# Own messages of a graph layer: from their own matmuls to scaled rows of x added to the slot sums in PSUM

## The chip, the core and the metric

The kernel runs on one core of a Trainium2 chip. The metric is device microseconds from the first to the last instruction of that core, as the hardware profiler takes it. The engines are called PE (matrix unit), PEld (its weight loads), DVE (vector), ACT (scalar), POOL (general, here the issuer of gathers) and SP (here the issuer of plain DMAs).

## The reference

N = 50,000 nodes carry rows of D = 160 numbers (64 scalars, 32 vectors of three). E = 1,650,000 edges have a source, a target and NK = 4 attributes. The edges are sorted by target, and each node has exactly one edge to itself among them, its "own" edge: 50,000 of the 1,650,000. A message is bilinear in the source's row and the edge's four attributes; messages are summed by target, mixed by two small matrices, and the layer ends in a residual, a relu and a layer norm:

```
out0 = C0 * (ss * e0 @ W1 + dot * INV3 @ W2)
...
m_agg = segment_sum(m, dst, num_segments=n)
hs = m_agg[:, :64] @ Ws * LIN_S
...
h  = concat([hs, hv])
x  = layernorm(x + x + relu(h))
```

Because a message is linear in the source's row for each attribute, the whole of it is the sum over k of attribute k times (row of x) times a fixed 160 x 160 matrix B_k, into which the W's are folded. So rows of x scaled by an attribute may be summed by target first, once for each k, and be multiplied by B_k afterwards.

## The kernel before, in words

**Edges and slots.** The sorted edges are cut into units of 128. G = 6 units make a group, whose targets span at most W = 32 consecutive nodes from the group's base (its first target). A group's sums live in one half of a PSUM tile ps: 128 partitions are 4 attributes x 32 slots, the 160 columns are the features. Two groups are a pair (PG = 2), four groups a chunk (QG = 4), 20 groups a super-chunk (SG = 20, ten pairs). There are 2,087 groups, 1,044 pairs, 522 chunks, 105 super-chunks and 391 blocks of 128 nodes.

**The main loop** runs over pairs. For each pair:
- POOL issues 12 indirect DMAs (gather, L324), each of which brings 128 rows of x into a slice of the tile xg. The pool of xg has four buffers of one pair, so POOL may run four pairs ahead of PE.
- DVE builds ha for the next pair (spread, L333 and L336): for each edge a one-hot over 32 slots times its four attributes.
- PE does 12 matmuls ps += ha^T xg (group_sums, L362). An f32 matmul appears as two weight loads and two passes.
- DVE transposes the finished ps by 32 x 32 blocks into the chunk's tile sums (turn_sums, L372), one pair later, after the second matmul of the next pair.

After a chunk, PE multiplies sums by the folded matrix in five matmuls (apply_weights, phc, L603), which gives 128 rows hp of the transformed sums by slot. When all chunks that can touch a block of 128 nodes are there, PE adds their hp to the block's nodes by one-hot matmuls (block, phb, L684), and DVE and ACT do the relu, residual and norm (L186 to L200). SP stores the output, two blocks at a time (L812).

**Own edges.** From the hundredth group on (head of 100 groups excepted), own edges are taken out of the edge list before gathering: "packs" of 128 long rows of raw edges are read, their own edges are found on DVE, the rest is squeezed together (many steps on DVE, L470 to L551), and SP writes it to a DRAM tensor edges. The four attributes of each node's own edge are written to a DRAM tensor selves, 4 numbers a node, at an address that is held in a register (put, L586). The super-chunks then read edges (load, L255).

The own messages come back in with the blocks. For each pair of blocks SP reads the rows of x (xt, L624) and their shares (sa, L628) seven pairs ahead of the chunk that completes the block. For each block PE transposes xt in two halves (turned, L650), ACT copies them to xT (L653), PE multiplies xT by the four B_k (own, yx, eight matmuls, L665), and DVE scales each product by its share and sums them up into t (L671, L673). At the end t is added to phb (L686).

**Order.** The order on SP, PE, DVE and ACT is that of the program text (manual_schedule). Work beside the 12 matmuls of a pair is held in a list of tasks with a first pair (after_pair, hand_over); after each matmul of the main loop, work(1.0) lets about one matmul's worth of tasks follow. The steps of a pack are spread evenly up to a due pair. PSUM tiles of phc, ptx, yx and phb share two buffers (psM, tag misc).

Of the kernel before, what the change touches and what calls it, by code (L numbers as in the profile page):

```python
# [50 lines left out]
P = 128  # L51
# [54 lines left out]
def tile_gnn_resnorm(ctx: ExitStack, tc: tile.TileContext, x, src, dst, attr, W1, W2, W3, W4, W5, Ws, Wv, out, n_edges):  # L106
# [104 lines left out]
    cuts = sorted({0, NH // QG, NCH} | {round(i * NCH / 10) for i in range(10)})  # L211
    bounds = []
    for c0, c1 in zip(cuts, cuts[1:]):
        t = min((near(c) / N for c in range(c0, c1 + 1)), key=lambda t: abs(t - 0.5))
        off = 5 * math.sqrt(n_edges * max(0, t * (1 - t))) / (degree - 1) + 10
        bounds += [(-off, 0.75 * step + W + off)] * (c1 - c0)
# [9 lines left out]
    with tc.tile_pool(name="once", bufs=1) as once, tc.tile_pool(name="raw", bufs=2) as rawp, \  # L226
# [4 lines left out]
            tc.tile_pool(name="ahead", bufs=5) as aheadp, tc.tile_pool(name="outs", bufs=3) as outp, \  # L231
# [3 lines left out]

        extremes = once.tile([P, 2, NSC], F32, name="extremes")
        baseB = once.tile([P, NCH * QG], F32, name="baseB")
# [41 lines left out]
        def place(cast_):  # L279
# [9 lines left out]
            nc.vector.tensor_scalar(baseB[:, gs], bank[:, 3, :ng], float(N - 1), None, op0=ALU.min)  # L289
            for g in range(QG):  # L290
                r = slice(g * W, (g + 1) * W)
                for c0, c1, h in ((s * SG // QG, (s * SG + ng) // QG, g),
                                  ((s * SG + ng) // QG, math.ceil((s * SG + ng) / QG), min(g, ng % QG - 1))):
                    if c0 < c1:
                        nc.vector.tensor_scalar(rowid[r, c0:c1],
                                                baseB[r, c0 * QG:c1 * QG].rearrange("p (c g) -> p c g", g=QG)[:, :, h],
                                                pidx[r], float(-g * W), op0=ALU.add, op1=ALU.add)
            yield 1
# [18 lines left out]
            placed[s] = si, rel, pk  # L317

# [51 lines left out]
        def turn_sums(ps, ng, at, i):  # L370

            nc.vector.transpose(at[:, :, i:i + ng, :].rearrange("p b g w -> p g b w"),  # L372
                                ps[:, :ng].rearrange("p g (b f) -> p g b f", f=FB))
# [14 lines left out]
        selves = dram.tile([1, (row_start(NR - 1)[1][1] + W) * NK], F32, name="selves")  # L388
# [4 lines left out]
        def row_table(tmp):  # L393
# [9 lines left out]
            nz = math.ceil((row_start(0)[1][1] + W) / P)  # L403
# [215 lines left out]
        def ahead(bs):  # L619
# [6 lines left out]
            assert rows_stored[0] == NR or row_start(rows_stored[0])[1][0] >= n1  # L626
            sa = aheadp.tile([P, BP, NK], F32, name="sa")
            dq.dma_start(sa[:nb, :len(bs)],  # L628
                         selves[0, n0 * NK:n1 * NK].rearrange("(h n k) -> n h k", h=len(bs), k=NK))
            return [(xt[:, h], sa[:, h]) for h in range(len(bs))]  # L630
# [11 lines left out]
        H = D // 2  # L642

        def turned(b, xt, sa):

            nb, row = rows_of(b)
            pt = psM.tile([H, 2, P], F32, name="ptx", tag="misc")
            fresh("misc")
            for i in range(2):
                wrote("misc", nc.tensor.transpose(pt[:, i, :nb], xt[:nb, i * H:(i + 1) * H], ident[:nb, :nb]))  # L650
                yield 0.75
            xT = np_.tile([H, 2, P], F32, name="xT")
            evict(xT[:, :, :nb], pt[:, :, :nb])  # L653
            return xt, sa, xT

        def own(b, xt, sa, xT):

            nb, row = rows_of(b)
            t = aheadp.tile([P, D], F32, name="t")
            for h in range(NK // 2):  # L660
                y = psM.tile([P, 2, D], F32, name="yx", tag="misc")
                fresh("misc")
                for k in range(2):
                    for i in range(2):
                        wrote("misc", nc.tensor.matmul(y[:nb, k], xT[:, i, :nb], BWh[:, i, 2 * h + k, :],  # L665
                                                       start=i == 0, stop=i == 1))
                        yield 1
                for i in range(2):
                    k = 2 * h + i
                    if k == 0:  # L670
                        nc.vector.tensor_scalar(t[:nb], y[:nb, i], sa[:nb, 0:1], None, op0=ALU.mult)  # L671
                    else:
# [425 lines left out]
```

## Time and profile before

| | |
|---|---|
| median of 3 runs | 18,558.09 us (18,557.72 to 18,613.09) |
| profiled execution | 18,571.46 us |
| its span | 18,569.1 us, mean granted PE clock 0.665 |
| PE busy | 8,634.2 us (46%), 41,633 passes |
| PEld busy | 7,746.4 us (42%), 41,634 |
| DVE busy | 6,447.4 us (35%), 11,070 |
| ACT busy | 486.0 us (3%) |
| POOL busy | 11,887.8 us (64%), 12,536 |
| DMA | 797,538 packets, 1,215.93 MB, mean 65 GB/s; software queue 20.7% of 16 engines, SP's queue 3.3% |

A row of the page's fifth part reads: line, engine, operation, tile written <- tiles read, count | busy us in total, mean ns of one | idle us of that engine just before them, and what ended the most of it ("issue": nothing that the profile shows; "remote": a semaphore whose raiser it can't name). A row of a timeline reads: start in us, duration in us, engine, line, operation, tiles, count, and in brackets the engine's idle time before it. SPq are issues of DMAs by SP; SP's register moves and loads are not in the page's busy time. Utilization is even over the span: in each of the 40 slices PE shows 4 or 5 tenths, POOL 6, DMA 2.

### The profile page before, as it was taken

How to read it: one execution, taken by the hardware profiler on the slowest of the kernel's cores; microseconds unless marked ns; L12 is line 12 of the kernel's file. 1: busy time of each engine (PE TensorE's matmuls, PEld its weight loads, DVE VectorE, ACT ScalarE, POOL GpSimd, SP SyncE). 2: the span in 40 equal slices, each digit the busy share in tenths (PEclk: the TensorE clock that was granted, in tenths of full speed). 3: DMA queues.
4: the chain of work that ended last, by engine and by line, in shares of the span. 5: the costliest groups of instructions: out<-in, count | busy, mean ns of one | idle time of the engine just before them, and what ended most of it. 6: DMA issues, size and time to landing. Idle time of an engine off the chain costs nothing.

```text
span 18569.1 us, 122717 instructions
## 1 busy us (share of the span) xinstructions
PE 8634.2 (46%) x41633; PEld 7746.4 (42%) x41634; DVE 6447.4 (35%) x11070; ACT 486.0 (3%) x1392; POOL 11887.8 (64%) x12536
## 2 busy tenths in 40 slices
PE   4444444444444444444445444455444444444444
PEld 3434444443443444444344444444444444344434
DVE  4332433423333233332333334233342423324222
ACT  0000000000000000000000000000000000000000
POOL 6666666666666666666666666666666666666665
PEclk6666666666666666666666666666666666666666
DMA  2222222222222222222222222222222222222222
GB/s 69 71 61 71 63 65 67 62 71 60 66 69 61 72 62 67 67 63 70 61 65 70 62 71 63 72 63 66 70 63 71 61 71 61 63 69 61 65 62 54
DMA packets 797538, 1215.93 MB, mean 65 GB/s; under 512 B 271491, under 2 KB 575800, under 8 KB 792918
## 3 DMA queue, kind: packets, MB, share of 16 engines
q0 software_dynamic: 601056, 1026.60, 20.7%
q1 hardware_dynamic: 194410, 180.15, 3.3%
q8 instruction: 330, 5.41, 0.1%
q14 instruction: 302, 2.47, 0.0%
q10 hardware_dynamic: 1440, 1.29, 0.0%
HBM read 1135.77 MB, written 71.40 MB: 65 GB/s over the span
## 4 chain that ended last, share of the span: by engine, by line
another core or an unknown queue 41%; issue 18%; PE 17%; DVE 10%; POOL 9%; ACT 1%; DMA 1%; DVEq 0%; SPq 0%; ACTq 0%; POOLq 0%
PE ps L362 9%; POOL xg L324 9%; PE phb L684 3%; DVE ha L336 2%; PE phc L603 2%; PE yx L665 2%; DVE hot L333 1%; DVE prow L534 1%; DVE sums L372 1%; DMA xg<-in_x,si 1%; DVE t L673 1%; DVE hot L638 0%; PE ptx L650 0%; DVE t L671 0%
## 5 line engine op out<-in xcount | busy, mean ns | idle before, releaser
L324 POOL DMA_INDIRECT xg<-in_x,si x12522 | 11883.6, 949 | 6638.9 <-issue 3628.4
L362 PE MATMUL ps<-xg,ha 128*128 128x160 f32 x25044 | 6522.3, 364 | 3418.1 <-issue 3062.0
L362 PEld LDWEIGHTS ps<-xg,ha 128*128 128x128 f32 x25044 | 5110.6, 241 | 3852.5 <-issue 3457.2
L372 DVE STREAM_TRANSPOSE sums<-ps 128x320 f32<-128x320 f32 x1044 | 534.2, 512 | 5451.7 <-remote 4041.4
L665 PE MATMUL yx<-BWh,xT 80*128 80x160 f32 x6256 | 1792.5, 364 | 880.7 <-issue 824.7
L684 PE MATMUL phb<-hp,hot 128*128 128x160 f32 x3474 | 1151.0, 422 | 2225.5 <-ACT xT L653 1099.2
L603 PE MATMUL phc<-BWk,sums 128*128 128x160 f32 x5220 | 1353.5, 343 | 1065.3 <-DVE t L673 534.0
L336 DVE TENSOR_TENSOR ha<-hot,pk 128x1536 f32<-128x1536 f32 x1044 | 1830.2, 1753 | 35.7
L684 PEld LDWEIGHTS phb<-hp,hot 128*128 128x128 f32 x3474 | 854.3, 280 | 2342.9 <-ACT xT L653 1144.9
L665 PEld LDWEIGHTS yx<-BWh,xT 80*128 80x128 f32 x6256 | 1344.0, 241 | 1004.7 <-issue 942.0
L603 PEld LDWEIGHTS phc<-BWk,sums 128*128 128x128 f32 x5220 | 1020.7, 225 | 1128.2 <-DVE t L673 563.5
L673 DVE SCALAR_TENSOR_TENSOR t<-yx,sa,t 128x160 f32<-128x160 f32 x1173 | 449.5, 383 | 2274.5 <-remote 1734.2
L671 DVE TENSOR_SCALAR t<-yx,sa 128x160 f32<-128x160 f32 x391 | 148.6, 380 | 1917.8 <-remote 1692.6
L650 PE MATMUL ptx<-ident,xt 128*80 128x128 f32 (+1 forms) x782 | 202.6, 351 | 1294.2 <-DVE t L673 982.2
L686 DVE TENSOR_TENSOR phb<-phb,t 128x160 f32<-128x160 f32 x391 | 128.1, 328 | 1687.3 <-remote 1000.5
L650 PEld LDWEIGHTS ptx<-ident,xt 128*80 128x80 f32 (+1 forms) x782 | 92.6, 142 | 1374.0 <-DVE t L673 1038.2
L333 DVE TENSOR_TENSOR hot<-bank,rel 128x384 f32<-128x384 f32 x1044 | 551.5, 528 | 34.1 <-PE ps L362 31.8
L534 DVE COPY_PREDICATED prow<-marks,prow 128x2370 f32<-128x2370 int32 (+8 forms) x160 | 445.9, 2787 | 1.2
L607 ACT COPY hp<-phc 128x160 f32<-128x160 f32 x522 | 152.8, 293 | 9795.3 <-remote 5044.4
L653 ACT COPY xT<-ptx 80x256 f32<-80x256 f32 x391 | 143.9, 368 | 8133.0 <-remote 4941.6
L534 DVE COPY_PREDICATED pra<-marks,pra 128x1580 f32<-128x1580 int32 (+8 forms) x160 | 306.5, 1915 | 0.0
L300 PE MATMUL bank<-ident,r 120*128 120x120 f32 x100 | 46.0, 460 | 542.0 <-DVE baseB L289 398.3
(144 smaller groups left out, 3035.8 us busy)
## 6 DMA issues: line engine op xcount, KB each, us to landing
xg<-in_x,si POOLq DMA_INDIRECT x12522
edges<-prow SPq DMA_DIRECT2D x1994, 18.5 KB
r<-edges SPq DMA_DIRECT2D x99, 360.0 KB
selves<-mine SPq DMA_DIRECT2D x1992, 0.5 KB
xt<-in_x SPq DMA_DIRECT2D x195, 160.0 KB
out<-o SPq DMA_DIRECT2D x195, 160.0 KB
pra<-in_attr SPq DMA_DIRECT2D x15, 1580.0 KB
pri<-in_src SPq DMA_DIRECT2D x15, 395.0 KB
```

The lines of the kernel that those rows point to most:

```text
L324: got.append(nc.gpsimd.indirect_dma_start(out=xg[:, j, :], out_offset=None, in_=x, in_offset=bass.IndirectOffsetOnAxis(ap=placed[0][:, u + ...
L333: nc.vector.tensor_tensor(hot[:, :n], slotsP[:, 0:W].unsqueeze(1).to_broadcast([P, n, W]), rel[:, u:u + n].unsqueeze(2).to_broadcast([P, n ...
L336: nc.vector.tensor_tensor(ha[:, :n], hot[:, :n].unsqueeze(2).to_broadcast([P, n, NK, W]), pk[:, :, u:u + n].rearrange("p k u -> p u k").un ...
L362: mm = nc.tensor.matmul(ps[:, j // G, :], ha[:, j].rearrange("p k w -> p (k w)"), xr, start=j % G == 0, stop=j % G == G - 1)
L372: nc.vector.transpose(at[:, :, i:i + ng, :].rearrange("p b g w -> p g b w"), ps[:, :ng].rearrange("p g (b f) -> p g b f", f=FB))
L534: nc.vector.copy_predicated(what[:n, a:e], mi[:, r].unsqueeze(2).to_broadcast([n, e - a, what.shape[2]]), what[:n, a + d:e + d])
L603: wrote("misc", nc.tensor.matmul(ph[:ng * W], at[:, b, :ng].rearrange("p g w -> p (g w)"), BWk[:, b, :], start=b == 0, stop=b == ND - 1))
L607: evict(hp[:ng * W], ph[:ng * W])
L650: wrote("misc", nc.tensor.transpose(pt[:, i, :nb], xt[:nb, i * H:(i + 1) * H], ident[:nb, :nb]))
L665: wrote("misc", nc.tensor.matmul(y[:nb, k], xT[:, i, :nb], BWh[:, i, 2 * h + k, :], start=i == 0, stop=i == 1))
L673: nc.vector.scalar_tensor_tensor(t[:nb], y[:nb, i], sa[:nb, k:k + 1], t[:nb], op0=ALU.mult, op1=ALU.add)
L684: wrote("misc", nc.tensor.matmul(ph[:nb], hot2[:r, i, :nb], hp[:r], start=i == 0, stop=i == len(cs) - 1))
```

## The change

Own messages leave the blocks and join the groups. In ps, partition (k, w) holds attribute k times rows of x summed for the node base + w. The own message of that node is its share k times its row of x; so a tile xr whose partition (k, w) holds row base + w of x, four times over, scaled by a column that holds share k of node base + w, is just what has to be added to ps. A node may lie in two groups' spans; its share counts only in the last, that is where base + w is below the next group's base (keep_shares), and is zero in the column elsewhere.

- turn_sums first calls add_own: for each group of the pair one DVE operation ps = xr * share + ps, in PSUM, then the transpose as before.
- ask_near: at the end of the step of pair p, SP asks for xr of pair p + 2: one register load of two addresses, and for each group one DMA of 32 rows of x, broadcast to four copies. Four buffers.
- ask_shares: once per super-chunk SP loads the addresses and issues one DMA of 128 single numbers for each group, handed over five pairs into the super-chunk before; keep_shares on DVE follows two pairs later.
- bases, in place: three DVE operations per super-chunk that turn the bases into byte addresses; the registers are loaded from there.
- Gone: turned, own, the reads of sa, the sum t and its addition to phb. The reads of xt come two pairs ahead of the completing chunk instead of seven.
- The due pair of a pack is also held before the first shares that need it. One more check on the widest step between bases, and somewhat wider bounds for the last chunk.

In all the program issues 1,988 DMAs of xr, 1,988 of shares (at) and 1,294 register loads for them on SP, and 1,988 operations of add_own on DVE; it loses 3,128 matmuls yx, 782 transposes, 391 copies xT, 1,564 operations on t, 391 additions to phb and 196 reads of sa.

```diff
-            nc.vector.tensor_scalar(baseB[:, gs], bank[:, 3, :ng], float(N - 1), None, op0=ALU.min)
+            nc.vector.tensor_scalar(baseB[:, gs], bank[:, 3, :ng], float(N - W), None, op0=ALU.min)
...
+            bases(s)
...
+        def bases(s):
+
+            g0, g1 = s * SG, min(NG, (s + 1) * SG)
+            lo, hi = reach(g0)[0], reach(g1)[1]
+            f = idxp.tile([1, SG], F32, name="basef")
+            i = basep.tile([1, 2, SG], I32, name="basei")
+            nc.vector.tensor_scalar(f[:, :g1 - g0], baseB[0:1, g0:g1], float(lo), float(hi), op0=ALU.max, op1=ALU.min)
+            for t, width in enumerate((NK, D)):
+                nc.vector.tensor_scalar(i[:, t, :g1 - g0], f[:, :g1 - g0], float(4 * width), None, op0=ALU.mult)
+            bases_[s] = i
+
+        def at_base(s, t, u0, u1):
+            _, v = nc.values_load_multi_w_load_instructions(
+                bases_[s][0:1, t, u0:u1], engines=[ET.SP], min_val=0, max_val=(N - W) * 4 * (NK, D)[t],
+                skip_runtime_bounds_check_because="held within bounds")
...
+        def ask_shares(s):
+
+            g0, g1 = counted(s)
...
+            at = sharep.tile([P, SG + 1], F32, name="at")
+            runs = [(s - 1, SG - 1, SG)] if g0 < s * SG else []
+            runs += [(s, u, min(u + 10, g1 - s * SG)) for u in range(0, g1 - s * SG, 10)]
+            i = 0
+            for s_, u0, u1 in runs:
+                for v in at_base(s_, 0, u0, u1):
+                    dq.dma_start(at[:, i:i + 1].bitcast(U8),
+                                 self_bytes[ds(v, W * 4 * NK)].rearrange("(w k b) -> k w b", k=NK, b=4))
+                    i += 1
+            shares[s] = at
+
+        def keep_shares(s):
...
+            nc.vector.memset(kept, 0.0)
+            nc.vector.scalar_tensor_tensor(keep[:, :n], baseB[:, g0 + 1:g1 + 1], slot_of[:, 0:1], baseB[:, g0:g1],
+                                           op0=ALU.subtract, op1=ALU.is_gt)
+            nc.vector.copy_predicated(kept[:, :n], keep[:, :n], shares[s][:, :n])
...
+        def ask_near(p):
+
+            s, g, ng = pairs[p]
+            own = [i for i in range(ng) if g + i >= OWN]
+            if not own:
+                return
+            xr = nearp.tile([P, PG, D], F32, name="xr")
+            for i, v in zip(own, at_base(s, 1, g + own[0] - s * SG, g + ng - s * SG)):
+                rows = xbytes[ds(v, W * 4 * D)].rearrange("(w b) -> w b", w=W)
+                dq.dma_start(xr[:, i, :].bitcast(U8), rows.unsqueeze(0).to_broadcast([NK, W, 4 * D]))
+            near_[p] = xr
...
+        def add_own(p, ps):
+
+            s, g, ng = pairs[p]
+            xr = near_.pop(p, None)
+            for i in range(ng):
+                if g + i >= OWN:
+                    share = next(shares.pop((t, g + i)) for t in (s, s + 1) if (t, g + i) in shares)
+                    nc.vector.scalar_tensor_tensor(ps[:, i], xr[:, i], share, ps[:, i], op0=ALU.mult, op1=ALU.add)
...
-        def turn_sums(ps, ng, at, i):
-
+        def turn_sums(p, ps, ng, at, i):
+
+            add_own(p, ps)
             nc.vector.transpose(at[:, :, i:i + ng, :].rearrange("p b g w -> p g b w"),
                                 ps[:, :ng].rearrange("p g (b f) -> p g b f", f=FB))
...
-        def turned(b, xt, sa):
...
-        def own(b, xt, sa, xT):
...
-            nc.vector.tensor_tensor(ph[:nb], ph[:nb], t[:nb], op=ALU.add)
...
-            due.append((first - 1) * per - 1)
+            own = next(s for s in range(NH // SG, NSC) if i * RP and reach(min(counted(s)[1], NG - 1))[1] + W > row_start(i * RP)[1][0] or not i * RP)
+            due.append(min((first - 1) * per - 1, (own - 1) * per + 4))
...
-        AHEAD = 7
+        AHEAD = 2
...
-                after_pair(max(at - AHEAD + 3, START), do_turned, b)
-                after_pair(max(at - AHEAD + 5, START + 2), do_own, b)
...
+                if counted(s + 1)[0] < counted(s + 1)[1]:
+                    after_pair(p + 5, ask_shares, s + 1)
+                    after_pair(p + 7, keep_shares, s + 1)
...
-            turning = ps, ng, sums, g % QG
-            fetch(p)
+            turning = p, ps, ng, sums, g % QG
+            if p + 2 < len(pairs):
+                ask_near(p + 2)
```

## The prediction

> **What bounds the kernel now.** I read the page first, then the timelines of POOL, PE and SP in the middle of the run, then counted instructions between the stalls seen there. The page's rows:
>
> ```profile
> L324 POOL DMA_INDIRECT xg<-in_x,si x12522 | 11883.6, 949 | 6638.9 <-issue 3628.4
> L362 PE MATMUL ps<-xg,ha 128*128 128x160 f32 x25044 | 6522.3, 364 | 3418.1 <-issue 3062.0
> L665 PE MATMUL yx<-BWh,xT 80*128 80x160 f32 x6256 | 1792.5, 364 | 880.7 <-issue 824.7
> L673 DVE SCALAR_TENSOR_TENSOR t<-yx,sa,t 128x160 f32<-128x160 f32 x1173 | 449.5, 383 | 2274.5 <-remote 1734.2
> L686 DVE TENSOR_TENSOR phb<-phb,t 128x160 f32<-128x160 f32 x391 | 128.1, 328 | 1687.3 <-remote 1000.5
> ```
>
> The first row sets the floor. Its busy and idle time make 18,522 of the span's 18,569 us. A gather costs 0.949 us and, when nothing holds it, an "issue" gap of 3,628.4 us / 11,880 = 0.305 us: 12,522 x 1.254 = 15,703 us. The remaining 18,522 - 15,703 = 2,819 us are stalls of POOL. No saving on another engine is worth more than these 2,819 us, and the change leaves the 12,522 gathers alone. When do they occur? POOL's timeline, the gathers with a long wait:
>
> ```profile
> 8017.20 0.95 POOL L324 DMA_INDIRECT xg<-in_x,si  x1 [4.76 <-remote]
> 8051.93 0.95 POOL L324 DMA_INDIRECT xg<-in_x,si  x1 [4.68 <-remote]
> 8086.40 0.95 POOL L324 DMA_INDIRECT xg<-in_x,si  x1 [4.71 <-remote]
> ```
>
> Every 34.5 us, two pairs of groups, POOL stands 4.7 us at the first gather of a pair. It waits for one of the four buffers xg, which PE frees with a pair's last matmul. Nearly all of some 600 such stalls stand at that place. So PE is late; PE's timeline in the middle one of these cycles says how:
>
> ```profile
> 8042.91 0.42 PE L362 MATMUL ps<-xg,ha 128*128 128x160 f32 x1 [2.39 <-issue]
> 8045.01 0.42 PE L362 MATMUL ps<-xg,ha 128*128 128x160 f32 x1 [1.68 <-issue]
> 8047.84 0.42 PE L665 MATMUL yx<-BWh,xT 80*128 80x160 f32 x1 [2.40 <-issue]
> 8049.25 0.43 PE L665 MATMUL yx<-BWh,xT 80*128 80x160 f32 x1 [0.99 <-issue]
> ...
> 8052.04 0.74 PE L362 MATMUL ps<-xg,ha 128*128 128x160 f32 x2
> 8052.57 0.74 PE L665 MATMUL yx<-BWh,xT 80*128 80x160 f32 x2
> ```
>
> Until 8050 PE crawls: starts lie at multiples of 0.70 us, with no operand missing (its gathers had been issued some 40 us earlier). From 8051 it runs a pass each 0.27 us. DVE's transpose at 8051.69 waited for a PE group whose last matmul is recorded at 8033, so PE's completions were held too. The crawl ends about 4.3 us after POOL has stopped. SP is caught in it as well; its own timeline:
>
> ```profile
> 8245.75 0.23 SPq L586 DMA_DIRECT2D selves<-mine  x1
> 8246.07 0.36 SPq L586 DMA_DIRECT2D edges<-prow  x1
> ...
> 8255.75 0.69 SPq L586 DMA_DIRECT2D edges<-prow  x1
> 8257.16 0.70 SPq L586 DMA_DIRECT2D selves<-mine  x1
> ```
>
> What starts a crawl? Not an idle PE: most start in the midst of work. I counted instructions from the end of one crawl to the start of the next, in 197 such stretches: a straight fit gives each PE instruction 0.0071 and each SP instruction 0.0072 of a stretch, that is some 140 of either. Stretches with many on SP (mean 34) had 105 on PE; those with few (2) had 134. DMA packets weigh nothing in it. I take this as a budget of instructions per stretch: the cause is not shown, the count is.
>
> **The change part by part.** *PE.* It loses 3,128 matmuls of yx and 782 transposes: 6,256 + 782 matmul rows and as many weight loads, 14,076 of 83,267. Their busy time, 1,792.5 + 202.6 us, lies under POOL and is worth nothing directly. Also gone are PE's waits for the evicted xT and for t (rows of phb and ptx: some 1 ms each), which lie in the same shadow. *ACT* loses 391 copies of xT, 143.9 us, hidden.
>
> *DVE.* Out: 391 + 1,173 on t and 391 on phb, 148.6 + 449.5 + 128.1 = 726 us. In: 1,988 scaled additions on PSUM. No row has PSUM as both source and target with an SBUF operand; nearest is L673, 383 ns, same form and size: 761 us. Bounds are 328 ns (L686, in place in PSUM) and 405 (the normalization's L200, two operands from SBUF): 652 to 805 us. Per super-chunk eight or nine small operations at 0.15 to 0.28 us, about 0.2 ms over 105. Net +0.24 ms (0.13 to 0.28) on a DVE that is 35% busy. It lengthens the step from a group's last matmul to its transpose by 2 x 0.38 us per pair; PE has a whole pair to do meanwhile. Nothing on the path, if the rows are there.
>
> *SP and its queue.* In: 1,988 reads of x rows (82 KB each, four copies), 1,988 reads of shares (128 numbers of 4 bytes), 1,294 register loads, and a register move for each read; out: 196 reads of sa. Durations in the trace: a move 29 ns, the issue of xt 415 ns and of sa 485 ns (256 rows each), of a store 227 ns; a load of 16 registers 1.15 us, of one 0.36. So 3,976 x (0.26 to 0.52) + 1,294 x (0.36 to 0.7) = 1.5 to 3.0 ms on an SP that spends 2.8 ms now: hidden in 18.5 ms while it keeps up. It does pass r, xt, out and the packs' stores in one queue; r has some four pairs of lead, xt six, the others need none. The new reads have less: asked for two pairs ahead (x rows), two to three (shares). Behind a late one stand DVE's addition, the transpose and the next pair's spread, and behind that PE.
>
> *DMA engines.* The rows are 163 MB on 1,216. Here the Trainium skill speaks against the change. "DMA: Bandwidth & Descriptors", section "Rules for kernel authors", says that an outermost dimension below 16, such as a leading broadcast of c copies, confines a DMA to c engines; both new reads lead with 4. By the trace's packets, 640 bytes take 36 ns and small ones 9: 128 x 45 ns x 1,988 = 11.5 ms of engine time. Over 16 engines that is 0.7 ms each; by the rule four of them get 2.9 ms each, 15% above the 24% they have now. A read then lands 1.2 us later than a spread one, against a lead of two pairs. Either way not a bound; I add nothing.
>
> A second rule, "TensorE: Matmul & The Clock Gate", section "HAM oscillation", says that gaps throttle the clock; fewer matmuls leave more gaps. The granted clock is already 0.665. Were all of the 34,600 passes that stay at the half-clock pace of 0.266 us, they would take 9.2 ms; the sum stays the same.
>
> *The stalls.* PE and SP have 84,403 + 9,984 = 94,387 instructions now (PE's 1,137 semaphore waits included). Change: -14,076 on PE, +2 x 3,976 + 1,294 - 196 = +9,050 on SP: 89,361, 5.3% fewer. With a fixed budget per stretch the stalls fall in proportion: 2,819 x 0.053 = 149 us. Both ends: nothing, if a stall comes every two pairs because four buffers fill; and 2,819 x 0.169 = 476 us, if only PE's count matters. I take the middle one, for SP's weight was measured.
>
> **Sum.** The profiled execution took 18,571 us (span 18,569), 13 above the median of 18,558. 18,571 - 149 = 18,422; against the median 18,409. I say **18,410 us**, 0.8% faster.
>
> **Rivals.** *A, the budget, as above:* 18,410, own range 18,330 to 18,520. Chance 0.35.
>
> *B, PE is the matter.* If crawls depend on PE alone, 18,558 - 476 = 18,080; and if PE also gets through three pairs instead of two before a crawl, since its back-and-forth with ACT and DVE for own messages is gone, one stall of 4.7 us falls on three pairs: 1.6 us a pair in place of 2.7, 1,044 x 1.1 = 1.2 ms less, 17,400. For it: rows with millisecond waits on xT and t. Against it: over windows of six pairs, pair time shows no trend with yx passes (17.8 us at 5.3 passes a pair, 17.5 between 6.7 and 8, 18.3 at 8). Chance 0.17.
>
> *C, SP's queue becomes a stage: slower.* Once in ten pairs the shares of a super-chunk are asked for in one lump: 20 x 2 + 3 = 43 instructions, 10 us when SP is free, 43 x 0.70 = 30 us in a crawl, plus 2 us to land. DVE takes them two to three pairs on: 35 us at the mean pace, but 14 to 16 us when PE and DVE do two pairs in one burst. It decides once the lump outlasts that: then DVE stands some 16 us, and PE and POOL after it. In half of the 99 super-chunks that is 0.8 ms: 19,240 with A's gain; in all, 20,060. Packs' stores (33 instructions a step) ahead of the x rows do the same. For it: crawls fill half of the time. Against it: pairs in which SP has 16 stores, far more than the 4 new reads, take only 0.3 us longer (18.0 against 17.7). Chance 0.33.
>
> *D, no effect:* a stall is fixed by the four buffers and comes every two pairs anyway. 18,560. For it: 435 of 604 intervals between stalls are two pairs. Chance 0.15.
>
> **Range and chances.** A measurement of this kernel tells about 0.3%, 56 us, from no change. A falls nearly all to faster, B wholly, D to the same, C to slower but for a little: 0.50, 0.17, 0.33. The range, 17,500 to 19,350, leaves out B's end and C's full price, under 2 in 10.
>
> **What would show it.** Right if POOL's mean stays at 949 ns and its idle falls by about 150 us; if PE has 69,190 matmuls and loads and its crawls stay; if ps<-xr takes near 383 ns and doesn't wait for DMA. B shows as stalls three pairs apart. C shows as DVE's additions or the copy of the shares idle until a DMA of xr or at. The forecast is wrong at the root if the gathers themselves get slower, say by sharing four DMA engines, or if crawls vanish: then 15.7 ms is open.

## The result: 1.3% slower

The changed kernel took 18,816.49 us (median of 4 runs, 18,809.39 to 18,828.72), the kernel before 18,557.9 (4 runs, 18,546.59 to 18,613.09): ratio 1.0134, interval 1.0113 to 1.0155. The forecast was 18,410, faster. The page of the changed kernel, parts 2, 3 and 5:

```profile
DMA packets 1269269, 1379.65 MB, mean 73 GB/s; under 512 B 488595, under 2 KB 1047368, under 8 KB 1264614
...
q1 hardware_dynamic: 666106, 344.04, 6.9%
...
L417 POOL DMA_INDIRECT xg<-in_x,si x12522 | 11848.7, 946 | 6923.1 <-issue 3621.3
L455 PE MATMUL ps<-xg,ha 128*128 128x160 f32 x25044 | 6560.4, 380 | 8374.5 <-issue 6584.8
...
L410 DVE SCALAR_TENSOR_TENSOR ps<-xr,kept,ps 128x160 f32<-128x160 f32 x1988 | 769.8, 387 | 6932.8 <-remote 2488.4
```

Read the POOL row first, as before. A free gather costs 0.946 + 0.305 = 1.251 us, so the floor is 12,522 x 1.251 = 15,665 us; busy and idle make 18,771.8, and the difference is stalls: 3,107 us, against 2,819 in the kernel before. The whole loss is stall time of POOL (the floor itself is 38 us lower). The additions take 387 ns each. PE lost all its yx rows, yet its idle time of kind "issue", the crawl, grew. New on the page are the packets: SP's queue q1 went from 194,410 to 666,106.

By the gathers' start times the changed kernel has 592 stalls of 5.25 us in the mean where the kernel before has 605 of 4.66. Of 9 us or more there are 26 (405 us in all) in place of one (11 us), so the shorter ones fell, from 2,808 us to 2,702. Within the 45 us before 24 of the 26, DVE's longest wait for a transfer or for ScalarE had been at x rows or at the step that takes up the shares. One of them, in the timelines of DVE and then of POOL:

```profile
4103.69 0.39 DVE L410 SCALAR_TENSOR_TENSOR ps<-xr,kept,ps 128x160 f32<-128x160 f32 x1 [10.93 <-DMA xr<-in_x]
...
4121.68 0.39 DVE L410 SCALAR_TENSOR_TENSOR ps<-xr,kept,ps 128x160 f32<-128x160 f32 x1 [0.58 <-DMA xr<-in_x]
```

```profile
4130.27 0.95 POOL L417 DMA_INDIRECT xg<-in_x,si  x1 [0.30 <-issue]
4144.55 0.94 POOL L417 DMA_INDIRECT xg<-in_x,si  x1 [13.34 <-PE ps L455]
```

DVE stands 10.9 us for x rows that SP asked for at 4100.18, behind a pack's stores; POOL pays some 40 us later. The table of waits of the same kernel adds such places up (us in total, times, longest us):

```profile
POOL xg L417 <- PE ps L455: 2216.6, 359, 40.2
DVE ps L410 <- DMA xr<-in_x: 1634.5, 224, 33.1
...
DVE kept L382 <- DMA at<-selves: 469.1, 15, 45.7
```

That is rival C's sign, word for word. The experiments say that it is a part of the cause and not the whole.

### The profile page after: what moved, and what is told of

Read it like the earlier page. It is cut to its first block, busy times and chain, and to the rows that moved or that the text cites. A ratio compares the mean times of both kernels' runs of the same rounds, so it can differ in the third digit from the quotient of the medians.

```text
span 18809.7 us, 120151 instructions
## 1 busy us (share of the span) xinstructions
PE 7544.6 (40%) x34595; PEld 6677.7 (36%) x34596; DVE 6577.2 (35%) x11924; ACT 358.3 (2%) x1001; POOL 11853.5 (63%) x12540
## 5 line engine op out<-in xcount | busy, mean ns | idle before, releaser
L455 PE MATMUL ps<-xg,ha 128*128 128x160 f32 x25044 | 6560.4, 380 | 8374.5 <-issue 6584.8
L455 PEld LDWEIGHTS ps<-xg,ha 128*128 128x128 f32 x25044 | 5258.0, 252 | 9091.9 <-issue 7164.2
L410 DVE SCALAR_TENSOR_TENSOR ps<-xr,kept,ps 128x160 f32<-128x160 f32 x1988 | 769.8, 387 | 6932.8 <-remote 2488.4
L697 PE MATMUL phc<-BWk,sums 128*128 128x160 f32 x5220 | 1306.2, 327 | 854.8 <-issue 854.1
L186 DVE SCALAR_TENSOR_TENSOR y<-phb,xt 128x160 f32<-128x160 f32 x391 | 126.1, 323 | 3839.7 <-remote 1915.7
L739 PE MATMUL phb<-hp,hot 128*128 128x160 f32 x3474 | 973.8, 370 | 71.3 <-issue 70.0
L739 PEld LDWEIGHTS phb<-hp,hot 128*128 128x128 f32 x3474 | 772.9, 253 | 69.1 <-issue 67.3
L728 DVE TENSOR_TENSOR hot<-bank,rr 128x512 f32<-128x512 f32 (+2 forms) x391 | 293.4, 750 | 13.4
L292 PE MATMUL bank<-first,ones 120*128 120x20 f32 (+1 forms) x210 | 58.5, 356 | 384.5 <-issue 127.0
L292 PEld LDWEIGHTS bank<-first,ones 120*128 120x128 f32 (+1 forms) x210 | 48.6, 285 | 434.5 <-issue 141.1
L200 DVE TENSOR_SCALAR o<-y,mv,rstd 128x160 f32<-128x160 f32 x391 | 147.0, 376 | 14.3
## 6 DMA issues: line engine op xcount, KB each, us to landing
edges<-prow SPq DMA_DIRECT2D x1994, 18.5 KB
```

The lines of the kernel that those rows point to most:

```text
L200: nc.vector.tensor_scalar(o[:n], y[:n], mv[:n, 0:1], rstd[:n], op0=ALU.subtract, op1=ALU.mult)
L410: nc.vector.scalar_tensor_tensor(ps[:, i], xr[:, i], share, ps[:, i], op0=ALU.mult, op1=ALU.add)
L455: mm = nc.tensor.matmul(ps[:, j // G, :], ha[:, j].rearrange("p k w -> p (k w)"), xr, start=j % G == 0, stop=j % G == G - 1)
L697: wrote("misc", nc.tensor.matmul(ph[:ng * W], at[:, b, :ng].rearrange("p g w -> p (g w)"), BWk[:, b, :], start=b == 0, stop=b == ND - 1))
L728: nc.vector.tensor_tensor(hot2[:, :len(cs)], slotsP.unsqueeze(1).to_broadcast([P, len(cs), P]), rr[:, :len(cs)].unsqueeze(2).to_broadcast( ...
L739: wrote("misc", nc.tensor.matmul(ph[:nb], hot2[:r, i, :nb], hp[:r], start=i == 0, stop=i == len(cs) - 1))
```

## Experiments

Each set of runs was on one chip, together with runs of the kernel before, so the ratio is what compares across sets. The sets differ: the changed kernel itself gave 1.0134 in one and 1.0036 in another, so differences of under a per cent between sets are not read as facts. Sets A and D have no run of the changed kernel as it is. "Stalls" is POOL's busy plus idle time less 12,522 free gathers (the mean of a gather plus 0.305 us). e1, e3, e5 to e8, e11, e12, e14, e15 and e17 leave the own messages out of the sums; these runs only serve to time a part.

| set (before, us) | kernel | us | ratio [interval] | stalls, us |
|---|---|---|---|---|
| first (18,557.9) | changed | 18,816.49 | 1.0134 [1.0113, 1.0155] | 3,107 |
| A (18,512.93) | e1_own_gone | 17,983.76 | 0.9709 [0.9696, 0.9723] | 2,286 |
| A | e2_reads_only | 19,135.77 | 1.033 [1.0312, 1.0348] | 3,382 |
| A | e3_fixed_rows | 17,998.61 | 0.9716 [0.9703, 0.973] | 2,260 |
| A | e4_lead5 | 18,892.0 | 1.0202 [1.0186, 1.0218] | 3,159 |
| B (15,707.1) | e5_rows_only | 15,701.59 | 0.9997 [0.9988, 1.0005] | under 15 |
| B | e6_shares_only | 15,702.11 | 0.9997 [0.9989, 1.0005] | under 15 |
| B | e7_one_packet | 15,701.27 | 0.9996 [0.9988, 1.0005] | under 15 |
| B | e8_fixed_addr | 15,702.68 | 0.9997 [0.9989, 1.0006] | under 15 |
| C (18,570.43) | e10_after | 18,638.87 | 1.0036 [1.0022, 1.0049] | 2,941 |
| C | e11_one_packet | 18,193.4 | 0.9793 [0.9779, 0.9806] | 2,521 |
| C | e12_fixed_addr | 18,368.04 | 0.9892 [0.9877, 0.9907] | 2,663 |
| C | e9_on_act | 19,501.46 | 1.0503 [1.0488, 1.0517] | 3,799 |
| D (18,565.13) | e13_rows5 | 18,651.53 | 1.0044 [1.003, 1.0058] | 2,881 |
| D | e14_rows_only | 18,203.19 | 0.9803 [0.979, 0.9816] | 2,458 |
| D | e15_shares_only | 18,172.3 | 0.9785 [0.9772, 0.9798] | 2,432 |
| D | e16_by_pe | 18,280.4 | 0.984 [0.9826, 0.9853] | 2,536 |
| E (15,729.19) | e17_reads_unused | 15,723.5 | 0.9996 [0.9987, 1.0005] | under 15 |
| E | e18_after | 15,723.36 | 0.9996 [0.9987, 1.0005] | under 15 |

### What is gone, and what is new: e1, e2, e3

e1 is the changed kernel without the new reads and additions, that is with the removed work alone:

```diff
-            add_own(p, ps)
...
-            if p + 2 < len(pairs):
-                ask_near(p + 2)
...
-                    after_pair(p + 5, ask_shares, s + 1)
-                    after_pair(p + 7, keep_shares, s + 1)
```

> The changed kernel without anything that it adds: no reads of x rows or shares, no bases, no additions in PSUM. It leaves out the own messages altogether. Budget of instructions: PE and SP have 14,076 + 196 fewer than before, 15% of 94,387; POOL's stalls fall by 15% of 2,819 us, time 18,130 (18,050 to 18,250). Fixed cycle (a stall every two pairs whatever PE has to do): 18,560 within 60. Queue theory (the loss after the change is SP being late with x rows in the packs' store stretches, and PE's work is worth nothing): 18,560 within 60, and no stall of POOL above 12 us.

e2 is the kernel before with the change's reads (ask_shares, ask_near and the bases that they need) added, which nothing uses:

```diff
+                    after_pair(p + 5, ask_shares, s + 1)
...
+            if p + 2 < len(pairs):
+                ask_near(p + 2)
```

> The kernel before, with the change's reads on SP added (addresses, register loads, x rows, shares) and nobody reading what they bring; own messages are made as before. Budget of instructions: 9,250 more on SP, 9.8% of 94,387; stalls up by 276 us, time 18,835 (18,750 to 18,900). Queue theory: nobody waits for the reads, so 18,560 within 80; a store or a load behind them may be late, but they have lead. Fixed cycle: 18,560 within 60. If DMA engines or HBM were shared too thinly, gathers would grow from 949 ns.

e3 is e1 with the additions back, from a tile of zeros instead of the reads:

```diff
-            xr = near_.pop(p, None)
+            xr = fixed
...
+                    share = fixed_share[:, 0:1]
```

> The changed kernel with its additions in PSUM, but from one fixed tile of zeros and a fixed share of zero, with no reads on SP: the own messages are left out, PE's saving and DVE's cost are kept. Budget: as without own messages, 18,130 (18,050 to 18,250), since DVE hardly counts. Queue theory: 18,560 within 60. If DVE's 0.77 us more between a pair's last matmul and its transpose were the loss, this would stand 200 us or more above the kernel without own messages.

The POOL rows of e1 and of e2:

```profile
L416 POOL DMA_INDIRECT xg<-in_x,si x12522 | 11851.2, 946 | 6100.2 <-issue 3652.3
```

```profile
L389 POOL DMA_INDIRECT xg<-in_x,si x12522 | 11883.8, 949 | 7201.1 <-issue 3607.1
```

The gather's own time is the same within 3 ns; only the idle time moves, 1,100 us apart. The removed work alone wins 18,513 - 17,984 = 529 us. Put on the 14,076 PE instructions, that is 0.038 us for each: the budget had some 420 for them, and 476 as its upper end. (DVE's 2,346 operations and ACT's copies went with them; no run takes these apart.) The reads alone, which no instruction waits for, cost 623 us; e2 also has the small operations of the bases on DVE and the packs' earlier due pairs, of which e1 has the latter too. The additions cost 15 us: 17,998.6 - 17,983.8. So the change is a win of 529 and a loss of 600 or more, and the loss is in the reads. Win and loss leave 94 us, 0.5%; that is near what sets C and D show (1.0036 and, with one more buffer, 1.0044), while the first set had 259. The difference between those sets is not explained. That a stall comes at a fixed pace (rival D) falls: e1 and e2 would both have stood at 18,560.

### Is it that the reads come late? e4

Here the x rows are asked for five pairs ahead, the shares two pairs earlier:

```diff
-("near", 4)
+("near", 7)
...
-            if p + 2 < len(pairs):
-                ask_near(p + 2)
+            if p + 5 < len(pairs):
+                ask_near(p + 5)
...
-                after_pair(p + 4, do_place, s + 1)
+                after_pair(p + 2, do_place, s + 1)
...
-                    after_pair(p + 5, ask_shares, s + 1)
+                    after_pair(p + 3, ask_shares, s + 1)
```

> The changed kernel with x rows asked for five pairs ahead instead of two (seven buffers), the placing of a super-chunk two pairs earlier, shares asked for two pairs earlier. Queue theory: 26 stalls above 9 us (405 us together) go back to the usual 4.7 us, time 18,530 (18,480 to 18,600). Budget: the same number of instructions as the changed kernel, so only what lateness costs comes back; same number. Fixed cycle with a slower step on DVE: 18,820, no change.

Its table of waits:

```profile
POOL xg L417 <- PE ps L455: 2080.7, 311, 43.7
...
DVE kept L382 <- DMA at<-selves: 430.2, 17, 51.1
DVE ps L410 <- DMA xr<-in_x: 142.6, 28, 32.1
```

DVE's wait for x rows is 142.6 us, against 1,634.5 in the first set's changed kernel. Yet e4 stands 893 us above e3 of the same set, which has the same additions and no reads. A wait that was named as the releaser of stalls was taken away and the time did not come. Lateness of the x rows alone is not the cause. Lateness as such is not ruled out: the shares' waits stayed, and of e4's 23 stalls of 9 us or more (492 us), 13 followed a wait of DVE for the loads of edges, which SP's queue also brings:

```profile
DVE first L290 <- DMA r<-edges: 492.7, 16, 54.1
```

### Runs without stalls: e5 to e8

These take the reads apart, all without the additions: e5 leaves out ask_shares, e6 ask_near, e7 takes one piece per read in place of 128 (first diff), e8 fixes the addresses when the kernel is built (second).

```diff
-                dq.dma_start(xr[:, i, :].bitcast(U8), rows.unsqueeze(0).to_broadcast([NK, W, 4 * D]))
+                dq.dma_start(xr[0:1, i, :].bitcast(U8), rows[0:1])
...
-                    dq.dma_start(at[:, i:i + 1].bitcast(U8),
-                                 self_bytes[ds(v, W * 4 * NK)].rearrange("(w k b) -> k w b", k=NK, b=4))
+                    dq.dma_start(at[0:1, i:i + 1].bitcast(U8),
+                                 self_bytes[ds(v, 4)].rearrange("(w b) -> w b", b=4))
```

```diff
-            for i, v in zip(own, at_base(s, 1, g + own[0] - s * SG, g + ng - s * SG)):
+            for i in own:
+                v = reach(s * SG)[0] * 4 * D
...
-                for v in at_base(s_, 0, u0, u1):
+                for v in [reach(s_ * SG)[0] * 4 * NK] * (u1 - u0):
```

> The changed kernel without its additions (own messages are left out of the sums) and without the reads of the shares: only the 1,988 reads of x rows remain, and nothing waits for them. Measured beside it: 17,984 us with no read at all; about 18,790 us is worked out for both reads (18,816 less the 15 us of the additions), so the reads together cost some 800 us. Each read of rows moves 128 pieces of 640 bytes to 128 partitions. If the cost goes with the number of transfers or of SP instructions, half of it stays: about 18,390 us. If it goes with bytes, nearly all of it stays: about 18,780. If it goes with the pieces, half: 18,390. If a DMA to SBUF with long pieces is cheap and 4-byte pieces are dear, little stays: about 18,050.

> The same, the other half: only the 1,988 reads of shares remain (own messages are left out of the sums; nothing waits for the reads). Each moves 128 pieces of 4 bytes. Transfers, SP instructions or pieces as the cost: about 18,390 us. Bytes as the cost: within 10 us of 17,984. Four-byte pieces as the cost: about 18,730.

> The changed kernel without its additions (own messages are left out), with both kinds of reads issued as in the change, the same number of SP instructions and transfers, but each read takes one piece to one partition (640 bytes of one row, 4 bytes of one share) in place of 128. If what costs is SP's instructions or the number of transfers, nothing changes: about 18,790 us. If what costs is the pieces or the bytes that the reads put on the DMA engines beside the gathers, the cost goes: 17,990 to 18,050.

> The changed kernel without its additions (own messages are left out), both kinds of reads with all their 128 pieces, but from addresses fixed when the kernel is built, so that SP loads no addresses: some 4,000 SP instructions in place of 9,250 for the same 3,976 transfers. If SP's instructions cost, each alike: 17,984 + 800 x 4,000 / 9,250, about 18,330 us. If transfers, pieces or bytes cost: about 18,790.

Every one of them, and the kernel before with 15,707.1 us over 41 runs, ran at the floor of 15,703 us. The four say nothing on the reads, but much on the stalls. e18, below, is the changed kernel itself in such a set; its page:

```profile
L417 POOL DMA_INDIRECT xg<-in_x,si x12522 | 11872.3, 948 | 3822.6 <-issue 3566.2
L455 PE MATMUL ps<-xg,ha 128*128 128x160 f32 x25044 | 9500.7, 488 | 4682.2 <-DMA xg<-in_x,si 4430.0
```

Same program, gathers as long (948 against 946 ns), granted clock 0.616 against 0.638; but PE's idle time is now the wait for its gathers, not "issue", and POOL is hardly ever held (six stalls of over 1 us, 12 us in all). The crawl is not a property of the program alone: in some sets it isn't there, and then a change of this size off POOL can't be seen.

### What in the reads costs: e10, e11, e12, e9

e11 and e12 repeat e7 and e8 beside the changed kernel (e10). e9 is the complete change with its reads on ScalarE's queue:

```diff
-                bases_[s][0:1, t, u0:u1], engines=[ET.SP], min_val=0, max_val=(N - W) * 4 * (NK, D)[t],
+                bases_[s][0:1, t, u0:u1], engines=[ET.Activation], min_val=0, max_val=(N - W) * 4 * (NK, D)[t],
...
-                dq.dma_start(xr[:, i, :].bitcast(U8), rows.unsqueeze(0).to_broadcast([NK, W, 4 * D]))
+                nc.scalar.dma_start(xr[:, i, :].bitcast(U8), rows.unsqueeze(0).to_broadcast([NK, W, 4 * D]))
```

> The changed kernel itself, once more. In the runs of one chip the kernel before took 18,513 us, in those of another 15,707, which is the sum of its gathers with hardly a stall. On a chip of the first kind: 1.013 of the time before, some 18,760 to 18,820 us. On one of the second kind the gathers alone set the end, and the change can neither win nor lose: within 10 us of the time before.

> The changed kernel without its additions (own messages are left out), with both kinds of reads, the same number of SP instructions and of transfers, each of one piece in place of 128. On a chip on which the kernel before takes about 18,520 us: some 18,780 us if SP's instructions or the number of transfers cost; 17,990 to 18,050 if the pieces or bytes do. On one on which it takes 15,707: 15,700, which tells nothing.

> The changed kernel without its additions (own messages are left out), both kinds of reads with all 128 pieces from addresses fixed when the kernel is built: some 4,000 SP instructions in place of 9,250. On a chip on which the kernel before takes about 18,520 us: 18,330 if every SP instruction costs alike, about 18,780 if transfers, pieces or bytes do. On one on which it takes 15,707: 15,700, which tells nothing.

> The whole change, with its reads (addresses and transfers) issued by ScalarE in place of SP; the computation is complete. ScalarE is busy for 2% of the span. On a chip on which the kernel before takes about 18,520 us: if only SP's instruction stream is held up while gathers are under way, the reads' cost goes and about 18,000 us is left; if any engine's instructions are held up alike, or transfers, pieces or bytes cost whoever issues them, 18,750 to 18,850 stays. On one on which it takes 15,707: 15,700.

The POOL row of e10, and the pages of e11 and of e12:

```profile
L417 POOL DMA_INDIRECT xg<-in_x,si x12522 | 11851.3, 946 | 6755.3 <-issue 3617.4
```

```profile
q1 hardware_dynamic: 149226, 181.40, 3.2%
...
L417 POOL DMA_INDIRECT xg<-in_x,si x12522 | 11851.4, 946 | 6334.5 <-issue 3631.3
```

```profile
q1 hardware_dynamic: 666106, 344.04, 7.0%
...
L418 POOL DMA_INDIRECT xg<-in_x,si x12522 | 11847.7, 946 | 6479.8 <-issue 3625.1
```

With no own messages at all this set would stand at 0.9709 x 18,570 = 18,030 us. That is an estimate: the ratio is carried over from set A, and the changed kernel's own ratio moved by 1%, some 180 us, between sets. By it, e11, with all of SP's instructions and transfers and hardly a piece, stands 163 us above; e12, with all pieces and 43% of SP's new instructions, 338; the changed kernel 609. The comparisons inside the set don't need it: e12 lies 175 us above e11 though SP does less, so the pieces cost by themselves. e11 and e12 lie 445 and 271 below the changed kernel, but both also lack its additions, and so every wait of DVE for a read.

The stalls' lengths in the traces, one profiled run of each kernel, say what kind of time each part costs (e14 and e15, further down, have half of the reads each; e1, e14 and e15 are from sets A and D):

| kernel | SP's new instructions | reads x pieces | stalls of 9 us or more | all other stalls, us |
|---|---|---|---|---|
| e1 | none | none | 1, 40 us | 2,246 |
| e11 | 9,246 | 3,976 x 1 | 16, 361 us | 2,160 |
| e14 | 4,971 | 1,988 x 128 | 3, 82 us | 2,376 |
| e15 | 4,275 | 1,988 x 128 | 2, 53 us | 2,379 |
| e12 | 3,976 | 3,976 x 128 | 8, 112 us | 2,551 |
| e10 | 10,051, waits included | 3,976 x 128 | 24, 346 us | 2,595 |

The ordinary stalls go with the number of pieces: half of them cost some 130 us, all of them 305 to 350 over e1, and SP's instructions alone nothing. The long stalls go with SP's instructions: about 350 us with all of them, 53 to 112 with about half or less. Before 14 of e11's 16, DVE had stood for a step of a pack on ScalarE (marks), which follows the pack's loads from SP's queue:

```profile
DVE hit L564 <- ACT marks L563: 782.8, 15, 72.6
...
ACT prow L543 <- DMA pri<-in_src: 650.5, 11, 69.5
```

So a price for each of SP's instructions is not what e11 shows; it shows loads that come late behind them. That these waits make the long stalls is read from their order in time; no run took them away. In e2 the split is less clear: of its 32 long stalls (373 us), 20 are under 10 us and only two follow such a wait of DVE.

On ScalarE the same reads are worse by 863 us than on SP. The page of e9:

```profile
q1 hardware_dynamic: 141274, 180.10, 3.0%
...
q10 hardware_dynamic: 526272, 165.23, 3.7%
...
L417 POOL DMA_INDIRECT xg<-in_x,si x12522 | 11851.2, 946 | 7613.2 <-issue 3612.2
```

The pieces sit on another queue now, and POOL's idle time grew. It has 43 stalls of 9 us or more, 1,454 us; before 32 of them DVE's longest such wait was for xt or for the loads of edges, before six for a step of a pack that ScalarE does (marks). xt and edges are still on SP's queue, where the packs' stores (L680) now stood for ScalarE's reads. From the tables of waits, the last line from SP's own:

```profile
DVE y L186 <- DMA xt<-in_x: 1524.8, 23, 92.5
...
DVE first L290 <- DMA r<-edges: 978.7, 24, 86.6
...
SPq L680 <- DMA xr<-in_x: 1361.0, 114, 77.1
```

A queue of its own for the reads is no help when the stores on SP's wait for it.

### The halves, the buffers, and a cheaper form: e13 to e16

e14 and e15 repeat e5 and e6. e13 is the complete change with one more buffer for gathered rows, and one fewer for x rows to make room:

```diff
-name="rows", bufs=4
+name="rows", bufs=5
...
-("near", 4)
+("near", 3)
```

> The changed kernel with five buffers for the gathered rows in place of four (and three for the own rows in place of four, to make room); the computation is complete. GpSimd's stalls, some 2,900 to 3,100 us in the changed kernel, come at every second pair or so, when it waits for a row buffer. If a stall has a price of its own (about 5 us, whatever was done before it) and the buffers set how often it comes, five buffers mean fewer stalls, four fifths to two thirds of them: 600 to 1,000 us less, about 17,650 to 18,200 on a chip on which the kernel before takes about 18,550. If the stalls make up for the work that TensorE and SP can't do while gathers are under way, their sum stays: 18,600 to 18,820.

> The changed kernel without its additions (own messages are left out) and without the reads of the shares: only the 1,988 reads of x rows, 128 pieces of 640 bytes each. Worked out on a chip on which the kernel before takes 18,550 us: 18,010 with no read (0.9709 of it), some 18,620 with both. Half of the reads' cost if number counts (pieces, transfers or instructions), 18,300; nearly all of it if bytes count, 18,600; little if only the 4-byte pieces count, 18,080. On a chip without stalls it tells nothing.

> The same with only the 1,988 reads of shares, 128 pieces of 4 bytes each (own messages are left out). Half of the reads' cost if number counts, 18,300 us; none if bytes count, some 18,090 with the SP instructions' part; most of it if 4-byte pieces are the dear ones, 18,550.

e16 reaches the change's end with a quarter of the pieces. The 32 rows are read once, the 32 x 4 shares as 32 pieces; VectorE lays the shares out as a 32 x 128 one-hot, and one more matmul per group adds the product. The rows are asked for three pairs ahead instead of two:

```diff
+                dq.dma_start(xr[:, i, :].bitcast(U8), rows)
...
+                    dq.dma_start(at[:, i, :].bitcast(U8),
+                                 self_bytes[ds(v, W * 4 * NK)].rearrange("(w b) -> w b", w=W))
...
+                nc.vector.tensor_tensor(oh[:, i:i + n], ident[:W, :W].unsqueeze(1).unsqueeze(2).to_broadcast([W, n, NK, W]),
+                                        kept[:, a:b].unsqueeze(3).to_broadcast([W, n, NK, W]), op=ALU.mult)
...
+                    mm = nc.tensor.matmul(ps[:, i, :], hots_[p][:, i].rearrange("p k w -> p (k w)"), near_[p][:, i, :],
+                                          start=False, stop=True)
...
-            add_own(p, ps)
```

> The own messages another way; the computation is complete. A group's 32 rows are read once, to 32 partitions (32 pieces of 640 bytes), its shares as 32 pieces of 16 bytes, VectorE spreads the shares over a one-hot of 32x128, and one more matmul per group adds the product to the sums; the additions on VectorE go. Worked out on a chip on which the kernel before takes 18,550 us: 18,010 with no own messages, 160 for the reads with one piece each, a quarter of 430 for the pieces, 1,988 matmuls and weight loads at 0.037 us each, 147: about 18,430, below both kernels. If the number of transfers and SP instructions were all that counts, 18,620 + 147 = 18,770.

The page of e13 and that of e16:

```profile
L417 POOL DMA_INDIRECT xg<-in_x,si x12522 | 11884.6, 949 | 6699.7 <-issue 3619.1
```

```profile
q1 hardware_dynamic: 332122, 222.09, 4.4%
...
L430 POOL DMA_INDIRECT xg<-in_x,si x12522 | 11909.3, 951 | 6354.6 <-issue 3615.6
...
L477 PE MATMUL ps<-xr,oh 32*128 32x160 f32 x3976 | 1403.7, 430 | 1546.4 <-issue 817.6
```

The fifth buffer wins nothing that can be read: 1.0044, stalls 2,881 us, beside 1.0036 and 2,941 in set C; its forecast for stalls with a price of their own was 600 to 1,000 us less. So the sum of the stalls is not a matter of the buffers. This speaks for stalls that make up for work left undone while gathers run, and once more against D.

Over 0.9709 x 18,565 = 18,025 us, an estimate as in set C, the rows alone cost 178 and the shares alone 147. Within the set they are 31 us apart, nearly alike, though a read of rows moves 82 KB and one of shares 0.5 KB: bytes are not what counts, and neither are 4-byte pieces dearer. What both have in common is 128 pieces, a transfer and SP's instructions.

e16 beats both kernels: 0.984, 371 us below e13, the complete change in the same set, and 150 below its own forecast. PE has 3,976 more matmul passes there than in the change and as many weight loads, but SP's queue has half the packets. Its long stalls, 24 with 323 us, are like the change's; the others are down to 2,213 us. Not only the pieces differ from the change: the additions, the copies' leading dimension of 4 and the lead of only two pairs went too, so the win is not shown to be the pieces' alone.

### What stayed open: e17, e18

e17 is the changed kernel with its reads and no addition, e18 the changed kernel beside it.

```diff
-            add_own(p, ps)
...
-                    after_pair(p + 7, keep_shares, s + 1)
```

> The changed kernel with both kinds of reads as they are and no addition (own messages are left out): nothing waits for the reads. If the reads cost by the load alone, this stands within 0.2% of the changed kernel on the same chip (15 us of additions apart), some 18,590 to 18,800 us. If the additions' waits for late reads are a good part of it, it falls to the sum of the two halves measured one by one: 18,010 + 190 + 160 = 18,360.

> The changed kernel beside it on the same chip: 1.003 to 1.014 of the time before, by the two sets of runs so far; some 18,620 to 18,820 us where the kernel before takes 18,560, and no difference where it takes 15,707.

Both stand at the floor like the kernel before, as in set B. What they tell is e18's page above: there the change is worth nothing, 0.9996 with an interval of 0.9987 to 1.0005. The sum of the halves, 178 + 147 = 325 us, falls short of the 609 of e10. The table of stall lengths says in which stalls the missing 280 us lie: of some 340 us by the stalls, 250 are in long ones, which the whole change has and the halves hardly have. Whether they would stay in a set with stalls if no addition waited for the reads was to be told by e17 and is not; e11, with 361 us of them and no such wait, speaks for it.

## Why the prediction was wrong

**The failed step** is in "The stalls": "-14,076 on PE, +2 x 3,976 + 1,294 - 196 = +9,050 on SP: 89,361, 5.3% fewer", with an equal price for either and none for what SP's instructions move. By its own rate, 2,819 us / 94,387 = 0.030 us, PE's part was a win of about 420 and SP's a loss of about 270. Measured: a win of 529 (e1) and a loss of 623 (e2). That the change would be paid and earned in stalls of POOL held, and so did the sign of each term; the reads' term was too small by a factor of 2.3. Two terms that had been put at nothing stand in its place. "DMA packets weigh nothing in it": the pieces alone put 391 us on POOL's ordinary stalls (e12 against e11). "hidden in 18.5 ms while it keeps up": with all of SP's new instructions some 350 us lie in long stalls behind late loads (e11, e10). SP's instructions as such, the only term that was priced, add nothing to the ordinary stalls (2,160 us in e11, 2,246 in e1). Why the fit over the kernel before gave the packets no weight stays open (over stretches of two pairs there, the packets of SP's queue and SP's instructions correlate by only 0.15 to 0.2, so they could be told apart), and so does why pieces lengthen a stall.

Point by point:
- **The floor**, 15,703 us: right, and met within 0.2% by all seven kernels of sets B and E. That POOL's stalls bound all gain was right.
- **PE**: rival B's first number, 476 us for PE alone, was near the 529. Stalls three pairs apart were not what came of it: 65 of the 510 intervals between e1's stalls.
- **DVE**: 383 ns foreseen, 387 measured, and the whole of the additions costs 15 us when their data is there. (A row with PSUM as source and target and an operand from SBUF did exist, L686, but for another operation.)
- **SP**: issues were taken at 0.26 to 0.52 us; medians were 0.594 (rows) and 0.556 (shares). That alone is no bound; what stands behind these issues in the queue is, in the long stalls.
- **DMA engines**: "Either way not a bound; I add nothing". As engine time that is so: q1 takes 6.9% of sixteen engines. As a price it is wrong; the reads' pieces cost stall time at a load far from full. On the Trainium skill's "DMA: Bandwidth & Descriptors", "Rules for kernel authors": a pair's reads of rows, 256 packets of some 36 ns, take some 2.5 us in the changed kernel, so 3.7 packets are under way at a time, worked out from the packets' records. That agrees with the four engines that the rule gives to a leading dimension of 4. (The delay of such a read comes to 1.1 us by the forecast's own figures, not 1.2.) No run changed the confinement alone, so its share of the price is open.
- **The clock**: 0.638 against 0.665, lower, as was drawn from the Trainium skill's "TensorE: Matmul & The Clock Gate", section "HAM oscillation". No sign of a weight here: e1 is the faster kernel at 0.641, and e18 reaches the floor at 0.616.
- **Rival C** had the sign and a symptom of 1,634 us of waits. Its mechanism, SP's queue coming late, holds in part: 405 us of long stalls in the changed kernel. It is not the whole, for the pieces cost in ordinary stalls (e12), and e2 lost 623 us with nobody waiting for its reads. The size it named, 0.8 ms and more, did not come.
- **D** fell with e1, e2 and e13. That "crawls vanish: then 15.7 ms is open" happened, in sets B and E, to both kernels alike.

## What to carry to other kernels

A transfer that nobody waits for, on DMA engines that are under 30% busy, need not be free; here such reads cost 623 us. Put the reads alone into the kernel before, unused, and time them, ahead of building what needs them; then count pieces, not bytes. A wait that the profile names as the releaser of a stall is a candidate and no more until a longer lead has taken it away; then see which wait takes its place, for the next thing in the same queue may be late instead. Sort the stalls by length before explaining their sum: here two causes lay in two lengths. And when the bounding engine's stalls can't be explained from its program, run the unchanged kernel again elsewhere first: here they were 2.8 ms in some sets and nothing in others.

## What the runs showed that was not expected

- **The stalls come and go with the set.** The kernel before took 18,513 to 18,570 us in four sets and 15,707 and 15,729 in two, steadily within each, with gathers of the same length. What differs no run shows; sets B and C name the same chip number, so it need not be the chip.
- **The crawl goes with them.** PE's rows end their idle time with "DMA xg" there, with "issue" (6,584.8 us) where POOL stalls.
- **A read on ScalarE's queue** cost 863 us more than the same read on SP's.
